# Attention in a four-layer graph network: the 62 rows of the last chunk placed twice on the partitions, each copy for half of the nodes, in six of eight heads

## The chip, the cores and the metric

The kernel runs on one core of a Trainium2 chip. A core has five engines that follow their own instruction streams and wait for each other through semaphores: TensorE (PE, matrix products, with its weight loads shown as PEld), VectorE (DVE), ScalarE (ACT), GpSimd (POOL) and SyncE (SP, which here only issues DMA transfers). The metric is the device time of one execution in microseconds. The kernel before was run three times: median 1824.16 us, from 1823.45 to 1826.29.

## The reference, cut to what matters

A network of four layers over 2708 nodes with 512 features and one dense adjacency matrix. Each layer normalizes its input, applies a ReLU, aggregates over neighbours and adds the result to its input. The change is made in the third layer, graph attention with eight heads of 64 features:

```python
Wh = jnp.einsum('nd,hdo->hno', x, W)
f1 = jnp.einsum('hno,ho->hn', Wh, a1)
f2 = jnp.einsum('hno,ho->hn', Wh, a2)
e = jax.nn.leaky_relu(f1[:, :, None] + f2[:, None, :], negative_slope=ALPHA)
e = jnp.where(adj[None, :, :] > 0, e, NEG_INF)
attention = jax.nn.softmax(e, axis=-1)
h_prime = jnp.einsum('hnm,hmo->hno', attention, Wh)
out = jax.nn.elu(h_prime)
```

For every head and every pair of nodes there is a weight, the exponential of a leaky ReLU, masked by the adjacency. A row of the output is a weighted sum over neighbours, divided by the sum of the weights. ALPHA is 0.2.

## The kernel before

The 2708 nodes lie in 22 chunks m = 0 to 21 of R = 126 rows; the last has 62 (`last_rows`). In attention, a chunk of 126 *neighbours* lies on the partitions, and all nodes n lie along the columns. The work is a list of *steps*, one for each unit u and chunk m. A unit is a head over all 2708 columns (the six middle heads, u = 2 to 7), or a head over half of them (head 0 is u = 0 and 1, head 7 is u = 8 and 9). The exponential of a leaky ReLU of a sum is the larger of two products of exponentials. So with factors taken out, one instruction makes all weights of a step: the maximum of a row and a number per partition, times the mask.

In a step s:

- `load_wh` (L859, and L862 for the short chunk) has loaded `Wh` of three chunks into one of three `wh` buffers.
- `scale` (L872, L874), on ScalarE, makes `whs`: `Wh` times a number per partition `ef`, and, in steps where it is needed, that number again in a column of its own.
- `make` (L883), on VectorE, makes the weights `t`, fp32: the maximum of the row `rb` (the other node's exponential, the same row on all partitions) and the number `ec`, times the mask `vT`. There are four buffers for it (`TILES`).
- `compare` (L901), on ScalarE, in 13 of the 22 chunks (`BY_SIDE`: m mod 5 in 1, 3, 4; the last chunk is one) of the middle heads, finds by a steep sigmoid which of the two products was the larger, as bf16 `b` (two buffers). The sum of weights then comes from cheaper matmuls with `b`.
- `multiply` (L1066), on TensorE, adds to `av`, the weighted sums of 64 features, and in the other chunks to `sums`, the sums of weights. `multiply_sides` does `sums` from `b`, one step later. `four` issues each as four groups of matmuls, with 32 columns of output partitions each: for `av` two halves of the features by two halves of the nodes, for `sums` four quarters of the nodes. All accumulate over 22 steps in PSUM, three banks for `av` and two for `sums`. [...]the next head's `av` takes the three that are left, and its `sums` needs banks that the ended head's `av` has to free.
- `evict` (L1105, copies `out` on ScalarE; L1107, DMAs to `avT` and `sumT` on SP) does that after a head's last step. The `out` tiles share three buffers.

The source emits, for each s, `scale` and `make` of step s+3, `compare` of s+1, `multiply` of s, the sides of s-1, and then what `plan` holds for the step. `plan` has the load of a head's row `rb` (L840, on SP, 126 copies of 2708 values, 1332.8 KB) at the fourth step of the head before, and its exponential, in place, on ScalarE (L847) at the eighth. `rb` has two buffers, and the row of head u+2 goes where head u's row was. A scheduler then sets the order on each engine; each queue runs in that order. ScalarE needs another function table for the exponential than for the sigmoid; the switches stand as ACT_TABLE_LOAD.

```python
        if s + 3 < len(steps):
            scale(s + 3)
            make(s + 3)
        if s + 1 < len(steps):
            compare(s + 1)
        multiply(s)
        multiply_sides(s - 1)
```

Elsewhere, and touched only by where buffers lie: `arow` (two rows for the products before attention), `wfs` and `wfn` (weights of the last layer), `rest` (scratch), `b3` (the last layer's bias) and the casts `kt` (L1291), which make fp32r masks for the last layer's aggregation. `er` and its small DMA (L1170) make the exponentials on the nodes' side after the heads.

Of the kernel before, what the change touches and what calls it, by code (L numbers as in the profile page):

```python
# [8 lines left out]
F32 = mybir.dt.float32  # L9
# [5 lines left out]
AF = mybir.ActivationFunctionType  # L15
ALU = mybir.AluOpType
# [4 lines left out]
P = 128  # L21

R = 126

TAIL = 64
# [19 lines left out]
def fast_layers(  # L45
# [36 lines left out]
    nc = tc.nc  # L82
    N, D = x_in.shape
    H, _, O = w2.shape
    NC = -(-N // R)
    NF = D // P
    O1 = O + 1

    last_rows = N - (NC - 1) * R
# [30 lines left out]
    weights = ctx.enter_context(tc.tile_pool(name="weights", bufs=2))  # L120
    dram = ctx.enter_context(tc.tile_pool(name="dram", bufs=1, space=DRAM))

    common = ctx.enter_context(tc.tile_pool(name="common", bufs=2))
# [49 lines left out]
            nc.sync.dma_start(w[:, i], src[i * P : (i + 1) * P, :])  # L173
        return w

    def load_row(pool, src, name, tag=None):

        t = pool.tile([P, D], F32, name=name, tag=tag or name)
        nc.sync.dma_start(t, bass.AP(tensor=src.tensor, offset=src.offset, ap=[[0, P], [1, D]]))
        return t  # L180

# [165 lines left out]
    vT = []  # L347
# [5 lines left out]
    where = {c: (g, k) for g, cs in enumerate(groups) for k, c in enumerate(cs)}  # L353
# [63 lines left out]
    with ExitStack() as ring_ctx:  # L417
        ring = ring_ctx.enter_context(tc.tile_pool(name="ring", bufs=NC - 1, side="right"))
# [29 lines left out]
        with tc.tile_pool(name="l0", bufs=2) as wk:  # L448
            units = [(g, m) for g in range(len(groups)) for m in range(NC)]
            tiles, uppers, acc, sums, xs = {}, {}, {}, {}, {}  # L450
# [349 lines left out]
    S = 32  # L800

    cut = EARLY * R // 8 * 8
    units = [(h, 0, N) for h in range(H)]
# [5 lines left out]
    def by_side(u, m):  # L809
        return 0 < units[u][0] < H - 1 and m in BY_SIDE  # L810
# [7 lines left out]
    f12 = late.tile([P, NC, 2 * H], F32, name="f12")  # L818
    nc.gpsimd.memset(f12, 0.0)
    at_ctx = ctx.enter_context(ExitStack())  # L820
    at = at_ctx.enter_context(tc.tile_pool(name="att", bufs=1, reuse_waits="tile"))
    ef = at.tile([R, NC, H], F32, name="ef")
    ec = at.tile([R, NC, H], F32, name="ec")
    eb = at.tile([R, NC, H], F32, name="eb")
    parts = at.tile([R, NC * H * 8 + S], BF16, name="parts")
    nc.gpsimd.memset(parts, 0.0)
    parts_of = parts[:, : NC * H * 8].rearrange("p (m h k) -> p m h k", h=H, k=8)
    parts2 = at.tile([R, NC, H, 3], BF16, name="parts2")
    nc.gpsimd.memset(parts2, 0.0)
    one6 = at.tile([R, S], F32, name="one6")  # L830
    nc.gpsimd.memset(one6, 0.0)
    nc.gpsimd.memset(one6[:, 6:7], 1.0)
    row, weight, wh, whs, acc, sides, made = {}, {}, {}, {}, {}, {}, []
# [18 lines left out]
    def load_wh(s):  # L852
        u, m = steps[s]
        h = units[u][0]
        t = at.tile([R, GROUP, O], F32, name="wh", bufs=3)
        k = min(GROUP, NC - 1 - m)
        if k > 0:
            src = whd[m * R : (m + k) * R, h * O : (h + 1) * O]
            nc.sync.dma_start(t[:, :k], src.rearrange("(k p) o -> p k o", p=R))  # L859
        if k < GROUP and m + k == NC - 1:  # L860
            src = whd[(NC - 1) * R :, h * O : (h + 1) * O]
            nc.sync.dma_start(t[:last_rows, k], src)  # L862
        for j in range(GROUP):
            wh[u, m + j] = t[:, j]

    def scale(s):

        u, m = steps[s]
        h, q = units[u][0], rows(m)
        t = at.tile([R, O + S], F32, name="whs", bufs=4)  # L870
        by = ef[:q, m, h : h + 1]
        nc.scalar.activation(t[:q, :O], wh.pop((u, m))[:q], AF.Copy, scale=by)  # L872
        if not by_side(u, m):
            nc.scalar.activation(t[:q, O:], one6[:q], AF.Copy, scale=by)  # L874
        whs[s] = t

    def make(s):
        u, m = steps[s]
        h, lo, hi = units[u]
        q = rows(m)  # L880
        g, k = where[m]
        t = at.tile([R, N], F32, name="t2", bufs=TILES)
        ins = nc.vector.scalar_tensor_tensor(  # L883
            t[:q, : hi - lo],
            row[h][:q, lo:hi],
            ec[:q, m, h : h + 1],
            vT[g][:q, k, lo:hi],
            op0=ALU.max,
            op1=ALU.mult,
        )  # L890
        weight[s] = t
        made.append(ins.ins)

    def compare(s):

        u, m = steps[s]
        h, lo, hi = units[u]
        q = rows(m)
        if by_side(u, m):
            b = at.tile([R, N], BF16, name="b", bufs=2)  # L900
            nc.scalar.activation(  # L901
                b[:q, : hi - lo],
                weight[s][:q, : hi - lo],
                AF.Sigmoid,
                bias=eb[:q, m, h : h + 1],
                scale=STEEP,
            )
            sides[s] = b

    l2p = ctx.enter_context(ExitStack())  # L910
    pp = l2p.enter_context(tc.tile_pool(name="l2p", bufs=2, side="right", reuse_waits="tile"))
    ar = [load_row(pp, a, f"arow{i}") for i, a in enumerate((a1, a2))]

    products, firsts = {}, {}

# [19 lines left out]
    def sums2(c):  # L935
        n = rows(c)
        f = small.tile([P, 2, H], F32, name="f")

        with tc.issue_after(firsts[min(c + 1, NC - 1)]):
            for i in range(2):  # L940
                t = products.pop((c, i))
                nc.vector.tensor_reduce(f[:n, i, :], t[:n, :, : O // (1 + i)], AX.X, ALU.add)

        nc.vector.tensor_scalar(
            f12[:n, c, :],
            f[:n].rearrange("p i h -> p (i h)"),
            F_MAX + 1.0,
            -F_MAX - 1.0,
            op0=ALU.min,
            op1=ALU.max,  # L950
        )

    def row2(c):
        pf = ps.tile([P, R], F32, name="f_ps", tag="ps")
# [34 lines left out]
    e3_ctx = ctx.enter_context(ExitStack())  # L989
    e3 = e3_ctx.enter_context(tc.tile_pool(name="e3", bufs=2, side="right", reuse_waits="tile"))  # L990
    er = e3.tile([R, NC, H], F32, name="er", bufs=1)
    rest = e3.tile([R, NC, H], F32, name="rest", bufs=1)
    kept3, l3_weights = {}, []


# [62 lines left out]
    def sizes_of(u):  # L1058
        _, lo, hi = units[u]
        return (hi - lo) // 2, (hi - lo) // 4  # L1060

    def four(out, size, operands, s):

        for p, (a, b) in zip(out, pieces(size)):
            for j, (lhsT, rhs, part) in enumerate(operands):
                nc.tensor.matmul(  # L1066
                    p[j * S : (j + 1) * S, : b - a],
                    lhsT,
                    rhs[:, part * size + a : part * size + b],
                    start=(s % NC == 0),  # L1070
                    stop=(s % NC == NC - 1),
                )

    def multiply(s):
        u, m = steps[s]
        q = rows(m)
        half, quarter = sizes_of(u)
        if m == 0:
            acc[u] = [
                [ps.tile([P, 512], F32, name=name, tag="ps") for _ in pieces(w)]  # L1080
                for name, w in (("av", half), ("sums", quarter))
            ]
        t, w = weight.pop(s)[:q], whs.pop(s)[:q]
        cols = [w[:, a : a + S] for a in range(0, O + S, S)]
        four(acc[u][0], half, [(cols[j % 2], t, j // 2) for j in range(4)], s)
        if not by_side(u, m):
            four(acc[u][1], quarter, [(cols[2], t, j) for j in range(4)], s)

    def multiply_sides(s):

        if s in sides:
            u, m = steps[s]
            h, q = units[u][0], rows(m)
            b = sides.pop(s)[:q]
            at_col = (m * H + h) * 8
            w = parts[:q, at_col : at_col + S]
            four(acc[u][1], sizes_of(u)[1], [(w, b, j) for j in range(4)], s)

    def evict(u, which):
        h, lo, hi = units[u]  # L1100
# [11 lines left out]
    def split():  # L1112

        nc.scalar.mul(eb, ec, -STEEP * ABOVE)
        for i in range(2):
            e = ef
            if i:
                nc.vector.tensor_tensor(rest, ec, ef, ALU.mult)
                e = rest
            for k in range(3):  # L1120
                part = parts_of[:, :, :, 3 * i + k]
                nc.scalar.copy(part, e)
                if k < 2:
                    nc.vector.tensor_tensor(rest, e, part, ALU.subtract)
                    e = rest
        heads = slice(1, H - 1)
        nc.scalar.copy(parts2[:, :, heads], parts_of[:, :, heads, 3:6])


    quarter = N // 4  # L1130
# [36 lines left out]

    def exp_nodes():
        nc.scalar.activation(er, f12[:R, :, :H], AF.Exp, scale=1.0 - SLOPE2)
        nc.sync.dma_start(er[TAIL : TAIL + last_rows, NC - 1], er[:last_rows, NC - 1])  # L1170

    def load_l3_weights():
        for i, name in enumerate(("wfs", "wfn")):
# [5 lines left out]
    def behind(s, fn, *args):  # L1179
        plan.setdefault(s, []).append((fn, args))  # L1180
# [9 lines left out]
    for u in range(2, len(units)):  # L1190
        if units[u][1] == 0:
            s = max(1, u - 1) * NC
            behind(s + 4, load_row1, units[u][0], 0, N)
            behind(s + 8, exp_row, units[u][0], 0, N)
    for u in range(len(units)):
        behind((u + 1) * NC - 1, evict, u, 0)
        behind(min((u + 1) * NC, len(steps) - 1), evict, u, 1)
    for i in range(len(BY_SIDE)):
# [39 lines left out]

    with ExitStack() as stack:
        ring = stack.enter_context(tc.tile_pool(name="ring3", bufs=NC - 1, reuse_waits="tile"))  # L1240
        b3 = e3.tile([P, D], F32, name="b3", bufs=1)
        nc.sync.dma_start(
            b3, bass.AP(tensor=bias3.tensor, offset=bias3.offset, ap=[[0, P], [1, D]])
        )
# [729 lines left out]
```

## Time and profile before

| what | value |
|---|---|
| median of three runs | 1824.16 us |
| profiled execution, its own time | 1825.62 us |
| span in the profile | 1823.8 us |
| PE busy | 1785.4 us (98%) |
| DVE busy | 1308.3 us (72%) |
| ACT busy | 796.6 us (44%) |
| POOL busy | 245.2 us (13%) |
| DVE `make` (L883), 220 instructions | 532.4 us |
| ACT `compare` (L901), 78 instructions | 199.0 us |
| ACT `scale` of `Wh` (L872), 220 instructions | 76.6 us |
| DMA, mean over the span | 97 GB/s |

In the profile, a group is a line of the code, an engine, an operation and the tiles that it writes and reads. Behind the bar come its busy time and the mean time of one instruction in ns, and behind the second bar the idle time of the engine just before, with what ended that idle time. In a timeline, the columns are the start and the length of a piece, both in us, the engine, the line and the operation; idle time before it stands in brackets. The chain of waits is followed back from the last instruction, in each step to what released it.

### The profile page before, as it was taken

Reading aid. Unit: us, or ns where it says so; the run is one execution under the profiler, and the core shown is the slowest. Engines: PE = TensorE matmul, PEld = TensorE weight load, DVE = VectorE, ACT = ScalarE, POOL = GpSimd, SP = SyncE. Lnnn points to the kernel's source line nnn. Section 1 sums busy time; section 2 is a strip of 40 time slices with the busy share of each in tenths; the row PEclk is TensorE's granted clock in tenths of the full one; section 3 lists DMA queues with packets and bytes.
Section 4 is the critical chain, followed back from the end, with each engine's and each line's share of the span. In section 5 each row is a group of like instructions: output and inputs, shape, how many; then the busy total and the mean of one; then the engine's idle time right before and its main releaser. Section 6 shows DMA issues by size and latency. Waiting matters only on the chain.

```text
span 1823.8 us, 30715 instructions
## 1 busy us (share of the span) xinstructions
PE 1785.4 (98%) x11884; PEld 1041.1 (57%) x11884; DVE 1308.3 (72%) x1836; ACT 796.6 (44%) x1542; POOL 245.2 (13%) x241
## 2 busy tenths in 40 slices
PE   9999999999999999999999999999999999999998
PEld 4456777654448887644544344334444445488776
DVE  4942998855446655788999999999989777533334
ACT  2632777731210000156896676776744566400000
POOL 0101323301110211266000000000000222100000
PEclk9999999999999999999999999999999999999999
DMA  7632666635462211353231121121012444313221
GB/s 247 193 112 67 204 209 199 193 80 115 116 143 58 71 57 46 94 149 104 73 89 35 33 61 41 29 61 53 15 36 53 130 139 131 95 34 109 82 68 45
DMA packets 165553, 176.62 MB, mean 97 GB/s; under 512 B 94830, under 2 KB 115792, under 8 KB 164516
## 3 DMA queue, kind: packets, MB, share of 16 engines
q1 hardware_dynamic: 143170, 131.47, 26.3%
q10 hardware_dynamic: 18484, 33.28, 5.3%
q0 software_dynamic: 3744, 9.82, 1.6%
q8 instruction: 95, 1.56, 0.4%
q14 instruction: 60, 0.49, 0.1%
HBM read 111.35 MB, written 55.15 MB: 91 GB/s over the span
## 4 chain that ended last, share of the span: by engine, by line
PE 77%; DVE 11%; DMA 5%; issue 4%; POOL 1%; ACT 1%; SPq 0%; ACTq 0%; DVEq 0%; POOLq 0%
PE acc L368 32%; PE av L1066 16%; PE nb_ps L184 6%; PE sums L1066 6%; DVE t L883 5%; PE self_ps L184 4%; PE wh_ps L184 3%; PE line_ps L184 2%; PE h_ps L184 2%; DVE cum L494 2%; PE fused_ps L312 2%; PE hT_ps L212 1%; DMA x<-x 1%; DMA rb<-rT 1%; DMA packed<-two 1%
## 5 line engine op out<-in xcount | busy, mean ns | idle before, releaser
L883 DVE SCALAR_TENSOR_TENSOR t<-rb,ec,vT 126x2708 f32<-126x2708 f32 (+2 forms) x220 | 532.4, 2469 | 20.6 <-PE sums L1066 10.9
L368 PE MATMUL acc<-halves,kt 126*126 126x512 f32 x1848 | 435.5, 395 | 3.7 <-DVE kt L741 2.1
L1066 PE MATMUL av<-t,whs 126*32 126x451 f32 (+3 forms) x4576 | 436.5, 515 | 0.6 <-DVE ln_mv L191 0.6
L368 PEld LDWEIGHTS acc<-halves,kt 126*126 126x126 f32 x1848 | 342.6, 186 | 93.1 <-DVE kt L741 6.5
L1066 PEld LDWEIGHTS av<-t,whs 126*32 126x32 f32 (+1 forms) x4576 | 160.2, 110 | 206.9 <-issue 181.7
L368 PE MATMUL acc<-halves,ar 126*126 126x512 f32 x924 | 235.4, 408 | 4.3 <-ACT ar L488 2.4
L901 ACT ACTIVATE b<-t,eb 126x2708 bf16<-126x2708 f32 (+1 forms) x78 | 199.0, 2551 | 21.2 <-DVE t L883 21.0
L368 PEld LDWEIGHTS acc<-halves,ar 126*126 126x126 f32 x924 | 171.0, 189 | 55.4 <-issue 8.1
L193 ACT ACTIVATE ln_rs<-ln_mv,eps 126x1 f32<-126x1 f32 x88 | 25.6, 293 | 341.1 <-DMA x<-x 199.2
L741 DVE SCALAR_TENSOR_TENSOR kt<-lastr,index,vT 126x504 fp32r<-126x504 int16 (+3 forms) x154 | 110.4, 728 | 80.9 <-PE acc L368 80.7
L1291 DVE CAST kt<-vT 126x504 fp32r<-126x504 uint8 (+3 forms) x154 | 55.9, 365 | 138.2 <-PE acc L368 138.2
L1066 PE MATMUL sums<-t,whs 126*32 126x338 f32 (+5 forms) x1568 | 140.5, 451 | 5.1 <-ACT out L1105 5.1
L872 ACT ACTIVATE whs<-wh,ef 126x64 f32<-126x64 f32 x220 | 76.6, 350 | 130.1 <-PE sums L1066 73.7
L1033 POOL TENSOR_SCALAR z<-y 126x512 f32<-126x512 f32 x22 | 44.0, 2000 | 664.8 <-DVE y L1026 656.0
L494 DVE TENSOR_TENSOR_SCAN cum<-ai,deg 126x504 int16<-126x504 int32 (+2 forms) x110 | 128.4, 1180 | 0.6 <-DMA ai<-in_adj 0.6
L522 ACT ACTIVATE cum<-cum,limit 126x504 int16<-126x504 int16 (+3 forms) x132 | 88.1, 667 | 59.9 <-DVE deg L502 58.9
L1066 PEld LDWEIGHTS sums<-t,whs 126*32 126x32 f32 (+1 forms) x1568 | 55.3, 109 | 73.1 <-issue 40.7
L189 DVE BATCH_NORM_STATS2 ln_st<-x 126x6 f32<-126x512 f32 x88 | 60.2, 685 | 45.7 <-DMA x<-x 30.8
L184 PE MATMUL h_ps<-w0s,hT 128*126 128x512 f32 x176 | 81.2, 605 | 4.7 <-ACT hT L214 3.5
L184 PE MATMUL nb_ps<-wfn,hT 128*126 128x512 f32 x176 | 80.7, 602 | 3.1 <-ACT hT L214 3.1
L184 PE MATMUL wh_ps<-w2s,hT 128*126 128x512 f32 (+1 forms) x176 | 79.4, 593 | 0.0
L184 PE MATMUL nb_ps<-wn,hT 128*126 128x512 f32 x176 | 79.2, 592 | 0.0
(182 smaller groups left out, 1870.6 us busy)
## 6 DMA issues: line engine op xcount, KB each, us to landing
x<-x SPq DMA_DIRECT2D x105, 252.0 KB
x<-x ACTq DMA_DIRECT2D x84, 252.0 KB
ai<-in_adj SPq DMA_DIRECT2D x84, 249.0 KB
x<-in_x SPq DMA_DIRECT2D x42, 252.0 KB
rb<-rT SPq DMA_DIRECT2D x7, 1332.8 KB
wh<-whd SPq DMA_DIRECT2D x70, 94.5 KB
packed<-two POOLq DMA_DIRECT2D x44, 124.5 KB, 4.5
whd<-wh SPq DMA_DIRECT2D x21, 252.0 KB
```

The source lines that it names most:

```text
L184: nc.tensor.matmul(po[:n], lhsT[:, f, :n], w[:, f, :], start=(f == 0), stop=(f == NF - 1))
L189: nc.vector.bn_stats(st[:n], xc[:n])
L368: nc.tensor.matmul(acc[:R], weight[:, k * R : (k + 1) * R], parts[:, i, :], start=(m == 0 and i == 0), stop=(m == NC - 1),)
L494: nc.vector.tensor_tensor_scan(cum[:n, :gw], ai[:n, :gw], ai[:n, :gw], 0.0 if g == 0 else deg[:n, m : m + 1], op0=ALU.add, op1=ALU.max,)
L522: nc.scalar.activation(cum[:n, :gw], cum[:n, :gw], AF.Sign, bias=limit[:n], scale=-1.0, accum_out=signs[:n, m, g : g + 1],)
L741: nc.vector.scalar_tensor_tensor(by_chunk(kt, cs), lastr[:, cs[0] * R : (cs[-1] + 1) * R].rearrange("p (c r) -> p c r", r=R), index[:R, m ...
L872: nc.scalar.activation(t[:q, :O], wh.pop((u, m))[:q], AF.Copy, scale=by)
L883: ins = nc.vector.scalar_tensor_tensor(t[:q, : hi - lo], row[h][:q, lo:hi], ec[:q, m, h : h + 1], vT[g][:q, k, lo:hi], op0=ALU.max, op1=AL ...
L901: nc.scalar.activation(b[:q, : hi - lo], weight[s][:q, : hi - lo], AF.Sigmoid, bias=eb[:q, m, h : h + 1], scale=STEEP,)
L1033: nc.gpsimd.tensor_scalar(z, y, 0.0, None, op0=ALU.min)
L1066: nc.tensor.matmul(p[j * S : (j + 1) * S, : b - a], lhsT, rhs[:, part * size + a : part * size + b], start=(s % NC == 0), stop=(s % NC == ...
L1291: nc.vector.tensor_copy(by_chunk(kt, cs), pattern(m, cs))
```

## The change

In the six middle heads, the 62 rows of the last chunk lie twice on the partitions, on 0 to 61 and on 64 to 125 (TAIL is 64, `second` is the upper part). The lower copy makes weights for the first 1354 nodes and the upper for the others, so that `make` and `compare` are one instruction over 126 partitions and 1354 columns for that chunk. Two tiles hold the inputs so arranged: `vp` for the mask, filled once, and `rp` for the row, filled for each head by two DMAs from `rb`. `Wh`, `ef` and so on need a copy on the upper partitions too: one DMA more and one `scale` more for that chunk. In `multiply` the same number of matmuls of the same sizes is issued, but those for the second half of the nodes read partitions 64 to 125. To make room, `arow` goes into the weights' pool, `rest` into the pool of the `out` tiles, and `b3` into the last layer's ring. The small DMA on `er` is replaced by one on `f12`.

```diff
@@ load_row
-        t = pool.tile([P, D], F32, name=name, tag=tag or name)
+        t = into
+        if t is None:
+            t = pool.tile([P, D], F32, name=name)
@@ ahead of the steps
+    half = N // 2
+    second = slice(TAIL, TAIL + last_rows)
+    vp = at.tile([R, half], mybir.dt.uint8, name="vp")
+    nc.gpsimd.memset(vp, 0)
+    rp = at.tile([R, half], F32, name="rp")
+    nc.gpsimd.memset(rp, 0.0)
+
+    def stack(dst, src):
+        nc.sync.dma_start(dst[:last_rows], src[:last_rows, :half])
+        nc.sync.dma_start(dst[second], src[:last_rows, half:N])
+
+    stack(vp, vT[where[NC - 1][0]][:, where[NC - 1][1]])
+
+    def stacked(u, m):
+        return m == NC - 1 and units[u][1:] == (0, N)
@@ load_wh
+            if stacked(u, NC - 1):
+                nc.sync.dma_start(t[second, k], src)
@@ scale
-        by = ef[:q, m, h : h + 1]
-        nc.scalar.activation(t[:q, :O], wh.pop((u, m))[:q], AF.Copy, scale=by)
-        if not by_side(u, m):
-            nc.scalar.activation(t[:q, O:], one6[:q], AF.Copy, scale=by)
+        w = wh.pop((u, m))
+        for own in (slice(0, q), second) if stacked(u, m) else (slice(0, q),):
+            by = ef[own, m, h : h + 1]
+            nc.scalar.activation(t[own, :O], w[own], AF.Copy, scale=by)
+            if not by_side(u, m):
+                nc.scalar.activation(t[own, O:], one6[own], AF.Copy, scale=by)
@@ make
+        w, f, v = hi - lo, row[h][:, lo:hi], vT[g][:, k, lo:hi]
+        if stacked(u, m):
+            q, w, f, v = R, half, rp, vp
         ins = nc.vector.scalar_tensor_tensor(
-            t[:q, : hi - lo],
-            row[h][:q, lo:hi],
-            ec[:q, m, h : h + 1],
-            vT[g][:q, k, lo:hi],
-            op0=ALU.max,
-            op1=ALU.mult,
+            t[:q, :w], f[:q], ec[:q, m, h : h + 1], v[:q], op0=ALU.max, op1=ALU.mult
         )
@@ compare
+            w = hi - lo
+            if stacked(u, m):
+                q, w = R, half
             nc.scalar.activation(
-                b[:q, : hi - lo],
-                weight[s][:q, : hi - lo],
+                b[:q, :w],
+                weight[s][:q, :w],
@@ before the steps, the two rows of the products
-    ar = [load_row(pp, a, f"arow{i}") for i, a in enumerate((a1, a2))]
+    arows = weights.tile([P, NF, D], F32, name="arows", tag="w")
+    ar = [load_row(None, a, None, into=arows[:, i]) for i, a in enumerate((a1, a2))]
@@ sums2
+        if c == NC - 1:
+            nc.sync.dma_start(f12[second, c], f12[:n, c])
@@ multiply (multiply_sides likewise, with w and b)
-        four(acc[u][0], half, [(cols[j % 2], t, j // 2) for j in range(4)], s)
+        if stacked(u, m):
+            own = [slice(0, q), second]
+            both = [(cols[j % 2][own[j // 2]], t[own[j // 2]], 0) for j in range(4)]
+            sums = [(cols[2][own[j // 2]], t[own[j // 2]], j % 2) for j in range(4)]
+        else:
+            both = [(cols[j % 2][:q], t[:q], j // 2) for j in range(4)]
+            sums = [(cols[2][:q], t[:q], j) for j in range(4)]
+        four(acc[u][0], half, both, s)
@@ split
+        rest = common.tile([P, D], F32, name="rest", tag="t", bufs=3)
+        rest = rest[:R, : NC * H].rearrange("p (m h) -> p m h", h=H)
@@ exp_nodes
-        nc.sync.dma_start(er[TAIL : TAIL + last_rows, NC - 1], er[:last_rows, NC - 1])
@@ plan
     for u in range(len(units)):
+        if stacked(u, NC - 1):
+            behind(u * NC + 3, lambda h: stack(rp, row[h]), units[u][0])
@@ last layer
-        b3 = e3.tile([P, D], F32, name="b3", bufs=1)
+        b3 = ring.tile([P, D], F32, name="b3", bufs=1)
```

More of the change, by code (lines that the diff above doesn't have):

```diff
@@ L174, in load_weight, with load_row @@
         return w
-    def load_row(pool, src, name, tag=None):
-        t = pool.tile([P, D], F32, name=name, tag=tag or name)
+    def load_row(pool, src, name, into=None):
+        t = into
+        if t is None:
+            t = pool.tile([P, D], F32, name=name)
         nc.sync.dma_start(t, bass.AP(tensor=src.tensor, offset=src.offset, ap=[[0, P], [1, D]]))
@@ L991, in fast_layers @@
     er = e3.tile([R, NC, H], F32, name="er", bufs=1)
-    rest = e3.tile([R, NC, H], F32, name="rest", bufs=1)
     kept3, l3_weights = {}, []
@@ L1082, in multiply @@
             ]
-        t, w = weight.pop(s)[:q], whs.pop(s)[:q]
+        t, w = weight.pop(s), whs.pop(s)
         cols = [w[:, a : a + S] for a in range(0, O + S, S)]
-        four(acc[u][0], half, [(cols[j % 2], t, j // 2) for j in range(4)], s)
+        if stacked(u, m):
[6 more added lines that the diff above has]
+        four(acc[u][0], half, both, s)
         if not by_side(u, m):
-            four(acc[u][1], quarter, [(cols[2], t, j) for j in range(4)], s)
+            four(acc[u][1], quarter, sums, s)
     def multiply_sides(s):
@@ L1093, in multiply_sides @@
             h, q = units[u][0], rows(m)
-            b = sides.pop(s)[:q]
+            b = sides.pop(s)
             at_col = (m * H + h) * 8
-            w = parts[:q, at_col : at_col + S]
-            four(acc[u][1], sizes_of(u)[1], [(w, b, j) for j in range(4)], s)
+            w = parts[:, at_col : at_col + S]
+            if stacked(u, m):
+                own = [slice(0, q), second]
+                sums = [(w[own[j // 2]], b[own[j // 2]], j % 2) for j in range(4)]
+            else:
+                sums = [(w[:q], b[:q], j) for j in range(4)]
+            four(acc[u][1], sizes_of(u)[1], sums, s)
     def evict(u, which):
```

## The prediction, made before the changed kernel was run

> **What bounds the kernel now.** I read the page first. TensorE is busy for 98% of the span, and the chain that ended last is PE 77%, DVE 11%, DMA 5%. So most of the time is matmul, but somewhere another engine sets the pace. The groups by form, from the trace, say how large the changed pieces are:
>
> ```profile
> L883 DVE SCALAR_TENSOR_TENSOR t<-rb,ec,vT 126x2708 f32<-126x2708 f32 x126 | 372.7, 3031 | 4.5 <-PE sums L1066 2.1 <-PE av L1066 1.8 <-ACT b L901 0.5
> L883 DVE SCALAR_TENSOR_TENSOR t<-rb,ec,vT 126x1384 f32<-126x1384 f32 x42 | 69.0, 1658 | 8.4 <-PE sums L1066 3.2 <-ACT rb L847 2.6 <-PE av L1066 1.1
> L883 DVE SCALAR_TENSOR_TENSOR t<-rb,ec,vT 62x2708 f32<-62x2708 f32 x6 | 18.2, 3027 | 0.0
> L901 ACT ACTIVATE b<-t,eb 62x2708 bf16<-62x2708 f32 x6 | 15.3, 2551 | 1.9 <-DVE t L883 1.9
> L847 ACT ACT_TABLE_LOAD x6 | 7.7, 1283 | 0.1
> ```
>
> 62 rows cost what 126 cost, and half the columns about half; so the six short chunks do shrink. Next the chain of waits over one middle head (1195 to 1280):
>
> ```profile
> by line: DVE t L883 43.7%; PE av L1066 22.1%; issue 14.6%; DMA rb<-rT 9.4%; PE sums L1066 9.2%; ACT out L1105 0.5%; ACT whs L872 0.4%; ACT whs L874 0.2%; DVEq L883 0.1%; ACTq L1105 0.1%; ACT rb L847 0.0%; ACTq L872 0.0%
> ...
> 1255.06 5.98 DVE t L883 x2
> 1261.06 7.99 DMA rb<-rT
> ```
>
> There the chain runs through VectorE, and at a head's end through the load of the next-but-one head's row `rb`, its exponential on ScalarE, and the copies `out` that free the PSUM banks. DVE's timeline has 86 of these instructions from 1019.03 for 253.81 us without a break: 2.951 each, 64.92 per head of 22. PE keeps the same pace: its `sums` of a new head start at 1008.33, 1076.09, 1140.93, 1205.85 and 1272.46. In these heads the waits show PE idle twice, 3.41 before 1008.33 and 1.67 before 1272.46, both for `ACT out`. The two engines are balanced, so what decides is the turn of a head. ScalarE's timeline there:
>
> ```profile
> 1195.01 0.33 ACT L872 ACTIVATE whs<-wh,ef 126x64 f32<-126x64 f32 x1
> 1195.25 0.30 ACT L874 ACTIVATE whs<-one,ef 126x32 f32<-126x32 f32 x1
> 1197.13 0.35 ACT L872 ACTIVATE whs<-wh,ef 126x64 f32<-126x64 f32 x1 [1.58 <-PE av L1066]
> 1197.40 2.55 ACT L901 ACTIVATE b<-t,eb 62x2708 bf16<-62x2708 f32 x1
> 1199.97 1.28 ACT L847 ACT_TABLE_LOAD   x1
> 1202.46 2.46 ACT L847 ACTIVATE rb<-rb 126x2708 f32<-126x2708 f32 x1 [1.21 <-DMA rb<-rT]
> 1204.83 0.33 ACT L872 ACTIVATE whs<-wh,ef 126x64 f32<-126x64 f32 x1
> 1205.07 0.31 ACT L874 ACTIVATE whs<-one,ef 126x32 f32<-126x32 f32 x1
> 1205.28 1.38 ACT L1105 COPY out<-av 128x451 f32<-128x451 f32 x3
> 1206.55 0.36 ACT L872 ACTIVATE whs<-wh,ef 126x64 f32<-126x64 f32 x1
> 1206.92 1.28 ACT L901 ACT_TABLE_LOAD   x1
> 1208.22 2.55 ACT L901 ACTIVATE b<-t,eb 126x2708 bf16<-126x2708 f32 x1
> ```
>
> The row load goes out at 1196.16 (SP's timeline), when DVE has ended the last chunk (m=21), because it overwrites the row that this instruction read. The last chunk's sigmoid and the exponential's table load lie under the transfer. From there: transfer 6.30, exponential to next 2.37, 0.24 and 0.21 for two scalings, 0.57 until PE starts: 9.69 to 1205.85.
>
> **What the Trainium skill says.** "ScalarE: Activation LUTs", What ACT_TABLE_LOAD costs: 1283 ns a load plus a drain; the trace agrees on the load (1283), and the next activation starts 1.30 after it, with no further drain seen. "TensorE: Matmul & The Clock Gate", Part 1: an idle window of some 3.4 us halves the clock, and the window runs free. The trace's clock records agree: half for 3.41 or 6.83, after PE idles of 2.60 (73.87), 3.41 (1004.92) and 3.14 (1425.17), and not after 1.67 (1270.79) or 1.83 (1412.19). "DMA: Bandwidth & Descriptors", Why a DMA increments its semaphore by 16 and not by 1: a transfer spreads over the largest number up to 16 that divides its outer size, so 62 rows use 2 engines, 126 use 14; the trace leaves 14 four-byte completion packets for a 126-row load and 2 for a 62-row one. "TensorEngine Tiling (Array Packing)", Gotcha 1: PSUM Pressure: different row tiles can't access one PSUM bank at the same time; before has no tile at row 64, so no run shows it.
>
> **The change, part by part.** Let E20 and E21 be the ends of DVE's rows m=20 and m=21 of a head.
>
> *DVE.* 126x1354, between 1.658 (1384 columns) and 1.597 (1324): 1.63 for 3.03, so 1.40 less per head, 8.4 over six. PE is as fast as DVE, so alone this could only shorten PE's waits.
>
> *The load of `rb`.* m=21 now reads `rp`, so the load waits for m=20 only (so the built program has it): it goes out at E20 = E21 - 1.63.
>
> *ScalarE's order.* In the built program the five turns with a row load now run: sigmoid of m=19, scaling, exp table load (it waits for the row), exponential, scaling, sigmoid table load, sigmoid of m=21, scaling and ones, the three `out`. So both table loads and the sigmoid stand behind the transfer and ahead of `out`. From E20: transfer 6.30, table 1.30, exponential 2.37, scaling 0.37, table 1.30 (both from the timeline above), sigmoid 1.28 (2551 less 1354 columns at 0.871 ns, which the exponentials of 1324 and 2708 columns, 1256 and 2462 ns, give: 1.37; the next starts 0.09 before the end). That is 12.92, E21 + 11.29. With 0.24, 0.21 and 0.57, PE's `sums` start at E20 + 13.94 = E21 + 12.31.
>
> *What is queued behind that sigmoid.* There are four weight buffers, and DVE's m=3 of the next head writes the one that m=21 used: it must wait for the sigmoid. m=0 to 2 end at E21 + 3 x 2.951 = 8.85; m=3 starts at 11.35, 2.5 late. Period: 11.35 + 18 x 2.951 + 1.63 = 66.10, where it was 64.92: **+1.18 per head**; the gain of 1.40 is inside it. First turn: E20 = 998.34 - 3.03 = 995.31, its transfer took 6.6, so `sums` at 995.31 + 14.24 = 1009.55, +1.2 on 1008.33. Four more periods: **+5.9** by the fifth turn. The sixth has no row load; later work keeps the shift, since PE runs on without gaps. Floor: the transfer now starts beside other traffic, 6.30 +- 0.5, so +3 to +8.
>
> *The clock.* Turns two to four leave PE idle some 1.2, below 1.83: nothing. At the fifth the load took 7.99 and PE idled 1.67; with 1.18 more it idles about 2.9, and in three of three cases from 2.6 up the clock halved: 3.41 us at half is **+1.7** (0 to 3.4).
>
> *`rp` copies,* two per head on SP behind `rb`, both on the same two engines. Per engine 62 packets of 5416 bytes. Lower bound 0.208 each (5536 bytes take 0.212 in the half rows): 12.9. Upper: `rb`'s nine packets of 10832 took 4.91 on an engine, so 0.273: 16.9. They start when `rb` and a `wh` are through, E21 + 4.8: end E21 + 17.7 to 21.7. The `avT` writes queue behind them, ScalarE's `out` of `sums` waits for those, and the sigmoid of m=3 stands behind it: ready at E21 + 21.6 to 25.6. DVE's m=7 wants that buffer at 11.35 + 4 x 2.95 = 23.2. So **0**, with 1.6 of cover; at the slow end 2.4 in each of five heads, +12. I take 0, as only two engines draw on memory there. The first head's copies (about 883) put off one `wh` load from 886.8 to about 898; before, its scaling ran at 893.68 and PE took it at 898.64, so PE may wait a little: +0.3 (0 to 3).
>
> *Matmuls.* Same number and sizes, in two row tiles of one bank: 0, or, if they take turns, a doubled m=21: 2.27 + 0.29 per head.
>
> *Moved buffers.* The last layer's bias leaves its pool, and its last casts `kt` (L1291) come ahead of the last chunk's work: PE's wait 1593.84 to 1595.23 goes, **-1.3** (0 to -1.4). The later `wfs` and `wfn` loads (about 857, first used after 1340), the two clears (POOL is idle from 763 to 773.8) and the `vp` copies (62 packets of 1354 bytes per engine, about 0.058 each by the 1520-byte packets' 0.065: 3.6, under loads with buffers to spare) are hidden; uncovered, the last would cost 3.6 once. The extra scaling of 62 rows (0.35) and the small copies come before E20, under ScalarE's idle time: 0.
>
> Sum: +5.9 + 1.7 + 0 + 0.3 - 1.3 = **+6.6**. It is made on the profiled span of 1823.8 (that run's own time 1825.62); the median of the runs is 1824.16, so span and median are alike and I predict 1831.
>
> **Rivals.**
> 1. *Copies late*: the slow end above, +12: 1843. For it: only two engines. Against it: the cover of 1.6, and idle memory. 0.2.
> 2. *Row tiles take turns*: PE would need 64.9 + 2.56 = 67.5 per head, 1.4 above DVE's 66.1: +1.4 x 5 on top, 1838. Against: the tiles write different partitions. 0.1.
> 3. *The turn half hidden* (a transfer of 5.7, 7.99 falling back to 6.3, no clock loss): +2.9 - 1.7 + 0.3 - 1.3, about 1824.5, no difference. 0.13.
> 4. *Faster*: the earlier row load decides. If it takes under 5.1 from E20 (6.30 - 1.18), the period falls below 64.92 and PE alone sets it; at 3.8 the first turn's wait shrinks by 1.4, the fifth's 1.67 goes, and 1.3 at `kt`: 1820. For it: it starts 3 us earlier than before. Against it: transfers of 6.3 to 8.0 in all five turns. 0.1.
> 5. *Nothing happens*, the shorter instruction being off PE's path: excluded as far as the chain over DVE and ScalarE's new order are real; inside 3.
>
> **From cases to numbers.** The likeliest has 0.47; its own range is 1827 to 1836. Slower takes it with rivals 1 and 2: 0.77; same 0.13, faster 0.10. A difference under 0.2% (3.6 us) can't be told from none here. The range leaves out rival 4 and what lies beyond late copies: 1822 to 1846.
>
> **What would show it.** Right: row loads issued at the end of m=20; ScalarE's two table loads both between the row's landing and `out`; DVE idle some 2.5 before the fourth instruction of a head, released by ACT `b`; turns 66.1 apart; half clock near the fifth turn; no wait for `kt` near 1600. Wrong: `out` of `sums` waiting on `avT` to E21 + 20 or later and DVE idle in mid-head (rival 1); a 62-row `av` of 4.5 us (rival 2); DVE without gaps at the turns (3, 4).

## The result and the profile after

The changed kernel took 1847.49 us (median of four runs, 1842.57 to 1849.05), beside 1825.22 for the kernel before on the same chip (1823.45 to 1829.12). The ratio is 1.0111, with a 95% interval from 1.0093 to 1.0129: slower by about 20 us. The profiled execution has a span of 1845.6, where it was 1823.8: 21.8 more. The direction of the prediction holds. On its scale (1.0111 times 1824.16) the time is 1844.4, inside its range of 1822 to 1846 but near the upper end; the median as it stands lies 1.5 above the range. Its size, +6.6, is a third of what came.

The groups by form after show that the shortened instructions are what was counted on, and who is waited for instead:

```profile
L909 DVE SCALAR_TENSOR_TENSOR t<-rb,ec,vT 126x2708 f32<-126x2708 f32 x126 | 373.3, 3035 | 21.1 <-ACT b L925 17.2 <-PE av L1092 2.4 <-PE sums L1092 1.0
L909 DVE SCALAR_TENSOR_TENSOR t<-rp,ec,vp 126x1354 f32<-126x1354 f32 x6 | 9.7, 1625 | 0.0
L925 ACT ACTIVATE b<-t,eb 126x1354 bf16<-126x1354 f32 x6 | 8.5, 1422 | 0.1
L866 ACT ACT_TABLE_LOAD x6 | 7.7, 1283 | 24.2 <-DMA rb<-rT 24.2
```

The six short steps fell from 3027 to 1625 ns on VectorE. But the wide ones now stand 17.2 us behind ScalarE's `b`, where 0.5 was shown before, and the table load ahead of the exponential waits 24.2 us for the row.

ScalarE's timeline at the turn that was shown of before (there 1195.01 to 1208.22):

```profile
1211.79 0.31 ACT L897 ACTIVATE whs<-one,ef 126x32 f32<-126x32 f32 x1
1216.66 1.28 ACT L866 ACT_TABLE_LOAD   x1 [4.56 <-DMA rb<-rT]
1217.95 2.46 ACT L866 ACTIVATE rb<-rb 126x2708 f32<-126x2708 f32 x1
1220.32 0.33 ACT L895 ACTIVATE whs<-wh,ef 126x64 f32<-126x64 f32 x1
1220.67 1.28 ACT L925 ACT_TABLE_LOAD   x1
1221.96 1.42 ACT L925 ACTIVATE b<-t,eb 126x1354 bf16<-126x1354 f32 x1
1223.29 0.33 ACT L895 ACTIVATE whs<-wh,ef 126x64 f32<-126x64 f32 x1
1223.53 0.31 ACT L897 ACTIVATE whs<-one,ef 126x32 f32<-126x32 f32 x1
1223.74 1.38 ACT L1143 COPY out<-av 128x451 f32<-128x451 f32 x3
```

ScalarE stands idle for 4.56 us, and then has both table loads, the exponential and the last chunk's sigmoid to do before `out`. VectorE's timeline of the same turn has the other side of it, a stop ahead of the fourth instruction of the head:

```profile
1209.19 1.63 DVE L909 SCALAR_TENSOR_TENSOR t<-rp,ec,vp 126x1354 f32<-126x1354 f32 x1
1210.94 8.96 DVE L909 SCALAR_TENSOR_TENSOR t<-rb,ec,vT 126x2708 f32<-126x2708 f32 x3
1223.42 53.20 DVE L909 SCALAR_TENSOR_TENSOR t<-rb,ec,vT 126x2708 f32<-126x2708 f32 x18 [3.52 <-ACT b L925]
```

TensorE's starts of `sums` at the turns are 1020.36, 1089.73, 1156.97, 1224.31 and 1291.60: the last three periods are 67.24, 67.34 and 67.29, where they should have been 66.10. And there is a loss that has nothing to do with these turns. The chain of waits near 900 begins with

```profile
887.02 16.24 DMA wh<-whd
```

and TensorE's waits between 770 and 930 are

```profile
PE adj_sums L1190 <- ACT x L1178: 5.0, 4, 3.9
PE wh_ps L186 <- ACT hT L216: 0.7, 1, 0.7
PE f_ps L982 <- DVE f L969: 0.4, 1, 0.4
```

(total, number, longest). The kernel before had only the last of them, 0.3. Here `x` is a bf16 cast of the mask, which ScalarE makes for the matmuls `adj_sums` that run between the others. Laid side by side by the start of each matmul, the two traces part in steps. From 785 to 790 the changed kernel falls 1.3 back, near 900 another 7.6 (5 us of waits and, with them, 6.83 us at half clock from 902.94). The five turns add 2.0, 1.6, 2.4, 2.4 and 0.7, and half the clock from 1292.06 for 3.41 us adds 1.6. What is left of 21.8 is 1.0 ahead of 770 and a balance of 1.1 behind the turns: up to 1458, where the changed kernel also runs at half clock from 1435.42 for 6.83 us, it falls 2.5 back, and near 1616 it gains 1.6, as the wait for `kt` is gone.

### The profile page after: what moved, and what is told of

Its sections match the earlier page's. It is cut to its first block, busy times and chain, and to the rows that moved or that the text cites. A ratio compares the mean times of both kernels' runs of the same rounds, so it can differ in the third digit from the quotient of the medians.

```text
span 1845.6 us, 30767 instructions
## 1 busy us (share of the span) xinstructions
PE 1792.1 (97%) x11884; PEld 1059.1 (57%) x11884; DVE 1302.2 (71%) x1836; ACT 791.0 (43%) x1548; POOL 247.2 (13%) x243
## 3 DMA queue, kind: packets, MB, share of 16 engines
q8 instruction: 95, 1.56, 0.3%
## 4 chain that ended last, share of the span: by engine, by line
PE 67%; DVE 12%; issue 8%; DMA 7%; ACT 2%; POOL 1%; SPq 0%; ACTq 0%; DVEq 0%; POOLq 0%
PE acc L370 31%; PE av L1092 14%; DVE t L909 5%; PE sums L1092 5%; PE nb_ps L186 4%; PE self_ps L186 4%; DMA x<-x 3%; PE wh_ps L186 2%; DVE cum L496 2%; PE h_ps L186 2%; PE fused_ps L314 2%; DMA rb<-rT 1%; DMA ai<-in_adj 1%; PE hT_ps L214 1%; POOL x L728 1%
## 5 line engine op out<-in xcount | busy, mean ns | idle before, releaser
L909 DVE SCALAR_TENSOR_TENSOR t<-rb,ec,vT 126x2708 f32<-126x2708 f32 (+2 forms) x214 | 515.9, 2456 | 46.4 <-PE sums L1092 17.7
L1092 PE MATMUL av<-t,whs 126*32 126x451 f32 (+3 forms) x4576 | 441.4, 517 | 0.6 <-DVE ln_mv L193 0.6
L1092 PEld LDWEIGHTS av<-t,whs 126*32 126x32 f32 (+1 forms) x4576 | 171.9, 110 | 198.2 <-issue 174.8
L925 ACT ACTIVATE b<-t,eb 126x2708 bf16<-126x2708 f32 (+1 forms) x78 | 192.2, 2464 | 18.0 <-DVE t L909 17.4
L1092 PE MATMUL sums<-t,whs 126*32 126x338 f32 (+5 forms) x1568 | 144.2, 455 | 14.5 <-ACT out L1143 14.5
L895 ACT ACTIVATE whs<-wh,ef 126x64 f32<-126x64 f32 (+1 forms) x226 | 78.9, 349 | 123.6 <-PE sums L1092 71.9
L1092 PEld LDWEIGHTS sums<-t,whs 126*32 126x32 f32 (+1 forms) x1568 | 60.5, 110 | 78.7 <-issue 36.2
```

The lines of the kernel that those rows point to most:

```text
L895: nc.scalar.activation(t[own, :O], w[own], AF.Copy, scale=by)
L909: ins = nc.vector.scalar_tensor_tensor(t[:q, :w], f[:q], ec[:q, m, h : h + 1], v[:q], op0=ALU.max, op1=ALU.mult)
L925: nc.scalar.activation(b[:q, :w], weight[s][:q, :w], AF.Sigmoid, bias=eb[:q, m, h : h + 1], scale=STEEP,)
L1092: nc.tensor.matmul(p[j * S : (j + 1) * S, : b - a], lhsT, rhs[:, part * size + a : part * size + b], start=(s % NC == 0), stop=(s % NC == ...
```

## The experiments

Three questions: is the loss in the copies on two DMA engines, or in ScalarE's order at the turn; are the turns what the prediction's sum says; and what is the change worth without either.

**Copies spread over the engines.** `move` is in the kernel: it sends 62 rows as 48 and 14.

```diff
     def stack(dst, src):
-        nc.sync.dma_start(dst[:last_rows], src[:last_rows, :half])
-        nc.sync.dma_start(dst[second], src[:last_rows, half:N])
+        move(nc.sync, dst[:last_rows], src[:last_rows, :half])
+        move(nc.sync, dst[second], src[:last_rows, half:N])
```

> Only the copies into rp and vp change: each of 62 rows goes out as 48 and 14 rows, so that 16 and 14 DMA engines share it instead of two. Theory A (the two-engine copies hold back what is queued behind them: the wh load that lands at 903.26, the x loads near 783): PE's wait of 3.9 us near 904 and the half clock after it go, as does the wait near 790; some 7.7 + 1.5 us less than the changed kernel, about 1838. Theory B (the whole loss is the turn of a head on ScalarE): the same as the changed kernel, 1847. Under both the turns stay near 67 us apart; if the copies also cause the row load's 7.35 us (6.30 before), it falls back to about 6.3 and the turns to 66.2, another 5 us less.

Measured: 1839.86, ratio to before 1.0083 (1.0062 to 1.0104). The waits near 904 and 790 are gone, as theory A has it, and ScalarE's waits for `avT` fell from 18.3 us to 0.4. But VectorE still waits for ScalarE at every turn (18.6 us in five), and the row doesn't land sooner: the spread copies now run amid its packets, 17 to 38 of theirs starting before its last has ended. So A is true, and is not all.

**ScalarE's order alone.** The exponential is queued behind the last chunk's sigmoid (`issue_after` puts an instruction behind another in the order).

```diff
+            if m == NC - 1:
+                compared[u] = ins.ins
...
+            elif fn is exp_row and steps[s][0] - 1 in compared:
+                with tc.issue_after(compared[steps[s][0] - 1]):
+                    fn(*args)
```

> Only ScalarE's order at the turn changes: the exponential of the row is queued behind the sigmoid of the last chunk, as in the kernel before, so that the table load and the sigmoid lie under the row's transfer. The copies stay on two engines. Theory B: the wait of VectorE for the sigmoid (3.5 us per turn) goes, turns fall from 67.3 to about 65, and 5 x 2.3 to 5 x 2.5 us are won, with the clock loss near 1292 some 13: about 1834. Theory A: no change at the turns, 1847. The wait near 904 stays under both.

Measured: 1843.3, ratio 1.0113 (1.0096 to 1.0129), not distinguishable from the changed kernel. That would have spoken against theory B, but the trace (of the fastest of the four executions, 1837.42) shows the place of the loss moved. ScalarE's timeline of one turn:

```profile
1226.28 0.44 ACT L1147 COPY out<-sums 128x338 f32<-128x338 f32 x1 [6.39 <-DMA avT<-out]
1226.93 0.44 ACT L1147 COPY out<-sums 128x339 f32<-128x339 f32 x1 [0.21 <-DMA avT<-out]
1227.27 0.35 ACT L895 ACTIVATE whs<-wh,ef 126x64 f32<-126x64 f32 x1
1227.52 2.54 ACT L927 ACTIVATE b<-t,eb 126x2708 bf16<-126x2708 f32 x1
```

`out` of `sums` comes sooner now, so it waits longer for the `avT` writes, which stand behind the row's copies on their two engines; a scaling and the sigmoid of the next head's m=3 stand behind it, and both TensorE (9.0 us in five waits, `av` for `whs`) and VectorE (16.2 us) wait for those. In the changed kernel ScalarE's late order had hidden that wait.

**Both edits.**

> Both edits: copies over 16 and 14 engines, and the exponential behind the last chunk's sigmoid. If A and B are both true and the rest of the change is free, what is left is the intended gain: the first turn 1.4 us earlier, the fifth turn's wait of 1.7 gone in part, the wait for kt gone (1.3 to 1.7): about 1821, faster than before by 0.1 to 0.3%. If a third cost exists (row tiles, the moved buffers, the wh load beside the row load), it stays above 1826.

Measured: 1815.74, ratio 0.9963 (0.9951 to 0.9976): faster than the kernel before. Of the 1.48% between the ratios of this and of the changed kernel, the first edit alone had given 0.28 and the second none. In the middle heads TensorE waits once, 1.3 us for `out` at the first turn (the second line stands ahead of them):

```profile
PE sums L1096 <- ACT out L1147: 1.3, 1, 1.3
PE f_ps L986 <- DVE f L973: 0.4, 1, 0.4
```

At the turns VectorE waits for TensorE alone, and its short step comes every 64.71 us (1124.91 to 1189.62), where a head took 64.92 before. So the shorter instruction buys some 0.2 us per head once TensorE sets the pace; the rest of the gain is waits that are gone. No run separates the shorter instruction from the row load that it lets out earlier.

**The moved buffers alone.** The last chunk isn't placed twice; `arow`, `rest` and `b3` stay moved and the copy of `f12` is kept; `vp`, `rp` and the copies into them are left out.

```diff
     def stacked(u, m):
-        return m == NC - 1 and units[u][1:] == (0, N)
+        return False
```

> Only the moved buffers (arow, rest, b3) and the 62-row copy of f12 are kept; the last chunk is not placed twice, and vp and rp are left out. The prediction's term: 1.3 us less than before, by the wait for kt near 1595 that goes: 1823. A rival: the later weight loads and the f12 copy cost as much or more, 1824 to 1826, with PE late by a microsecond between 780 and 900.

Measured: 1821.67, ratio 0.999 (0.998 to 1.0001), in line with the predicted 1.3 but not clear of nothing. So the moves cost nothing that shows, and most of what the run with both edits gains is the doubled chunk's.

**The row load behind the `wh` load.** The changed kernel with the load of `rb` queued behind the `wh` load that followed it. `loaded` holds the `wh` loads by unit and chunk. ScalarE's order is then that of the run with the order alone.

```diff
+            elif fn is load_row1 and (steps[s][0], 6) in loaded and steps[s][0] > 2:
+                with tc.issue_after(loaded[steps[s][0], 6]):
+                    fn(*args)
```

> The changed kernel with one edit: the row load of the next-but-one head is queued behind the wh load that stood right after it. The copies stay on two engines. By this alone the scheduler also puts the exponential behind the last chunk's sigmoid, so it is to be read beside the run with that order (1843). If the wh load's 378 packets of 256 bytes among those of the row are what stretched the row's transfer (4.9 to 5.0 us from first to last packet before, 5.6 to 6.0 after), it falls back to 5.0 at the later turns. If the copies or the earlier start are the cause, it stays at 5.6 or more. The time: within 5 us of 1843 either way, since the avT writes behind the copies hold the turn.

Measured: 1839.43, ratio 1.0076 (1.0056 to 1.0097). Without a single 256-byte packet amid them, the row's packets still take 5.2 to 5.5 us from the first to the last, against 4.9 to 5.2 in four of the five turns before and 5.0 to 5.9 in the changed kernel. So the `wh` load isn't the whole cause of the stretch.

**The same on top of both edits.**

> Spread copies, the exponential behind the sigmoid, and the row load behind the wh load. The run with the first two has one wait of TensorE left in these heads, 1.3 us at the first turn. If the turn there is set by the row's transfer, a transfer 1 us shorter takes most of that wait: about 1814.5 to 1815.5, no difference that a measurement can tell from 1815.7.

Measured: ratio 0.9971 (0.9963 to 0.9979), no better than both edits alone. TensorE waits 1.6 at the first turn.

**The first head's copies alone.** Only the mask's copies and those of the first middle head are spread.

```diff
-    stack(vp, vT[where[NC - 1][0]][:, where[NC - 1][1]])
+    stack(vp, vT[where[NC - 1][0]][:, where[NC - 1][1]], True)
...
-            behind(u * NC + 3, lambda h: stack(rp, row[h]), units[u][0])
+            behind(u * NC + 3, lambda h: stack(rp, row[h], h == 1), units[u][0])
```

> The changed kernel, with only the copies of the first middle head and those of the mask spread over 16 and 14 engines; the later heads' copies stay on two, and ScalarE's order stays. Theory A in its narrow form (the loss of the copies is the wh load of 903.26 and the x load near 783): 7.7 + 1.5 us less than the changed kernel, about 1838, and turns of 67.3 as there. If the later heads' copies cost as well in this order, spreading them all would have been worth more than this; the run that spread all has 1839.9.

Measured: 1838.23, ratio 1.0066 (1.0042 to 1.009). That is all, or nearly all, that spreading every copy had given: what spreading takes away is the cost at two places, the `wh` load near 900 and the mask near 785.

**Copies later, on two engines, and ScalarE's order.** Place against width.

```diff
+    def late_stack(u):
+        with tc.issue_after(loaded[u, 12]):
+            stack(rp, row[units[u][0]])
...
-            behind(u * NC + 3, lambda h: stack(rp, row[h]), units[u][0])
+            behind(u * NC + 7, late_stack, u)
```

> Copies on two engines, but queued four steps later in each head, behind the wh load of m = 12; the exponential behind the sigmoid. Place against width: if the two-engine copies cost only because of what stands behind them at a head's turn (avT writes, then the out copies of sums, then the scalings), they cost nothing here, and the time is that of the run with both edits, about 1816, with no wait near 904. If two engines are too slow wherever they stand (16 us against some 20 us of lead of a wh load), waits for wh appear in mid-head and the time stays above 1826.

Measured: 1818.71, ratio 0.9964 (0.995 to 0.9977), the same as with spread copies. Two engines are wide enough there; where the copies stood was the fault. Of the waits, one of TensorE at the turns is left, 1.0 at the first, and the mask's near 785:

```profile
PE wh_ps L186 <- ACT hT L216: 2.1, 2, 1.4
PE sums L1098 <- ACT out L1149: 1.0, 1, 1.0
```

**Copies later, ScalarE's order as changed.** The same edit without the order: the turn by itself.

> The changed kernel with only the copies of the row moved four steps later in each head; two engines, ScalarE's order of the changed kernel. This is the turn alone, without copies beside the row's transfer. By the prediction's own sum: transfer 6.3, turns 66.1 apart, TensorE idle about 1.2 at turns two to four, no half clock there, no wait near 904: the prediction's 1831. If the row's transfer keeps 7.3 (because it starts earlier, or by the wh load behind it), turns stay at 67.2 and the time is about 1837. If the order costs nothing without the copies, 1818, as in the run with both edits.

Measured: 1831.52, ratio 1.0039 (1.0025 to 1.0053). VectorE's timeline:

```profile
1133.25 1.63 DVE L911 SCALAR_TENSOR_TENSOR t<-rp,ec,vp 126x1354 f32<-126x1354 f32 x1
1134.99 8.96 DVE L911 SCALAR_TENSOR_TENSOR t<-rb,ec,vT 126x2708 f32<-126x2708 f32 x3
1146.57 53.19 DVE L911 SCALAR_TENSOR_TENSOR t<-rb,ec,vT 126x2708 f32<-126x2708 f32 x18 [2.62 <-ACT b L927]
1199.67 1.63 DVE L911 SCALAR_TENSOR_TENSOR t<-rp,ec,vp 126x1354 f32<-126x1354 f32 x1
1201.40 8.96 DVE L911 SCALAR_TENSOR_TENSOR t<-rb,ec,vT 126x2708 f32<-126x2708 f32 x3
1213.04 53.19 DVE L911 SCALAR_TENSOR_TENSOR t<-rb,ec,vT 126x2708 f32<-126x2708 f32 x18 [2.68 <-ACT b L927]
```

VectorE stops 2.4 to 2.9 us per turn (2.5 predicted), its short step comes every 66.4 (1133.25 to 1199.67; 66.1 predicted), TensorE idles 1.25 to 1.56 at the later turns (1.2 predicted), and the whole kernel is at the 1831 of the prediction. That the total agrees is in part luck: this trace is 2.9 late ahead of the first turn, where the sum has 0.3, and lacks the half clock at the fifth, for which the sum has 1.7. Between this kernel and the last lies only ScalarE's order (the other engines' instructions and the DMA issues stand in the same order in both traces): 1.0039 against 0.9964, intervals apart. So theory B is true as well.

**All that helped.** Late copies, spread, and the order.

> All that helped together: late copies, spread over 16 and 14 engines, the mask's too, and the exponential behind the sigmoid. Against the run with late copies on two engines (1818.7, ratio 0.9964) only the wait of 1.4 us near 785 goes, behind the mask's copies: ratio 0.995 to 0.997.

Measured: 1817.9, ratio 0.9964 (0.9951 to 0.9976). The wait near 785 is gone, and the time can't be told from that of the two-engine version. This, both edits, and late copies with the order all beat the kernel before by about 0.36%.

## Why the prediction was right in direction and short in size

*The turn of a head: right.* Its steps are all in the trace: the row load goes out at the end of m=20 (1209.31), both table loads stand between its landing and `out`, VectorE waits for the sigmoid of m=21 ahead of the fourth step. From the landing to TensorE's start the changed kernel takes 1216.66 to 1224.31, 7.65, for 7.64 in the sum. The run with late copies shows the term alone, at its size.

*The transfer in that turn: too short.* The sum took 6.30 from the kernel before. The five turns had 7.33, 7.12, 7.25, 7.35 and 7.31 from issue to the table load (1209.31 to 1216.66 in the one shown). With late copies it was 6.44 to 6.51 and the period 66.4; 0.9 more is the 67.3. From the first packet to the last, the turn shown has 5.92, and 4.91 before. With copies late and the same `wh` load behind the row, the span is 5.0 to 5.1; with the copies behind it and no `wh` load, 5.2 to 5.5; with both, 5.0 to 5.9. So the copies that are queued right behind are the larger part. The prediction allowed 0.5 for other traffic, but of the copies it had only asked when they would end, not what they do to the transfer ahead of them. By what mechanism is open: none of their packets starts before the row's last has ended (1216.39 and 1216.13 in the turn shown).

*The copies: the step that failed.* "+0.3 (0 to 3)" for the first head measured 7.6. The `wh` load was put off not to 898 but to 903.26. The changed kernel was 2.3 late by then, so in the time of the kernel before it landed at 900.9. The copies' packets were on the two engines until 902.51, 16.8 after issue, for a median of 0.208 us per packet as the lower bound had it, but with other loads in between. And the cover was smaller than the sum took it to be. It held the landing against TensorE's use of the scaled `whs`, five microseconds after the scaling. But TensorE first needs the casts `x`, which stand behind that scaling on ScalarE, and the last of these had a lead of 1.0. Before (L1138 is the cast, L1150 the matmul):

```profile
895.25 2.07 ACT L1138 CAST x<-vT 126x677 bf16<-126x677 uint8 x3
898.34 0.47 PE L1150 MATMUL adj_sums<-x,parts 126*24 126x338 bf16 x8
```

After:

```profile
903.35 0.35 ACT L895 ACTIVATE whs<-wh,ef 126x64 f32<-126x64 f32 x1 [7.25 <-DMA wh<-whd]
903.82 0.74 ACT L1178 CAST x<-vT 126x677 bf16<-126x677 uint8 x1
904.61 0.44 PE L1190 MATMUL adj_sums<-x,parts 126*24 126x338 bf16 x1 [3.88 <-ACT x L1178]
907.03 0.72 PE L1190 MATMUL adj_sums<-x,parts 126*24 126x338 bf16 x5 [0.21 <-ACT x L1178]
```

From the landing to the last of these waits is 3.77 (903.26 to 907.03). An estimate from these lines: a load landing at 898 would already have cost some 3.4 (901.8 against 898.4), the later landing adds 2.9, and the half clock 1.2, together the 7.6. For the mask's copies the uncovered value of 3.6 stood in the prediction, and the cover did not: VectorE waited 2.9 us for a load of the layer's input, and TensorE lost 1.3.

*The cover behind the later copies: right in the changed kernel, and by luck of ScalarE's order.* ScalarE waits 18.3 us for `avT`, but no VectorE step past m=3 waits for it. The kernel with the order put right shows what the cover was: TensorE's 9.0, and VectorE's stops, 16.2 in all, at the turn shown there ahead of the step m=7 that the prediction named.

*The clock: half speed came at the fifth turn, but by luck.* It came at 1292.06 after an idle of 2.38, not the 2.9 of the sum, and an idle of 2.41 one turn earlier brought none. Near 900 and at 1435.42 it was missed. The prediction's reading, half from 2.6 up and full speed at 1.83 and below, left out a record of its own trace, half from 359.39 after an idle of 1.88 that ended at 358.38.

*The rest.* TensorE's wait for `kt` is gone, as predicted. The two row tiles in one bank, which no run before could show, don't take turns: 48 matmuls that begin with the short chunk take 4.89 (1217.01), 4.90 before. Rival 1, late copies, had the cause of the largest single loss and the nearer total, 1843, but for the changed kernel at the wrong place: a `wh` load and not the sigmoid of m=3. Its place is where the run with the order alone loses. Rival 4 needed the row to land within 5.1: it never did. But the waits that it names are what the kernels with the right order save: about 6.6 by the ratios, where it had some 4, from the first turn (3.41 to 1.3 of wait, no half clock near 1008) and the fifth (no wait).

## What to carry to other kernels

An instruction made shorter on a balanced engine is worth only what waits it removes; ask first what the edit does to the order on the engines beside it. Here, freeing an input early let a scheduler lift a row's exponential over a sigmoid whose buffer VectorE wanted, and undid the gain. Cost a copy by what is queued behind it, at each place where it is issued. Follow the delayed load to the first instruction that another engine waits for, here a cast that stood behind it in a queue, and hold the delay against the lead of that one. And when two waits end at the same instruction, test them together: here one edit alone gave a fifth of the gain of both, and the other nothing.

## What the runs showed of the hardware that was not expected

- The clock halved after idles of TensorE well below 2.6: after 1.83 (`hT_ps` at 1434.78, half from 1435.42, the changed kernel), after 2.15 (`av` at 1227.67, the run with the order alone), after 2.29 (1146.08, the run with the first head's copies spread) and after 2.38 (1291.60, the changed kernel). It did not after 2.41 (1224.31, the changed kernel), 2.84 (1078.88, the first head's copies spread) and even 3.13 (1425.28, the moved buffers alone). No fixed length separates them.
- The fifth turn's row load took 7.99 in the kernel before and 7.95 with the moved buffers alone, at the same place, where the other turns of these kernels had 6.3 to 6.6. In the changed kernel it took 7.31, no more than at the turn ahead of it. Why is open.
